# Fourteen squarings of a power iteration, taken out of the first attention scores and dealt between the matmuls that enter the first batch

## The chip, the core and the metric

The kernel runs on one core of one Trainium2 chip. The metric is the device time of one execution in microseconds, the median of several runs. The engines that matter here are TensorE (PE in the profile; PEld is its weight load), VectorE (DVE), ScalarE (ACT), GpSimd (POOL) and SyncE (SP), which issues the DMAs. Each of them works through an instruction stream of its own, and the streams meet at semaphores.

## What is computed

The input is x, 8 images of 512 channels and 32 x 32 pixels, in float32. Four layers follow each other; each ends with the addition of its own input. Cut to what matters:

```python
# layer 0: attention whose scores are divided by their largest singular value
f = relu(batchnorm(conv1x1(x, Wf)));  g = relu(batchnorm(conv1x1(x, Wg)));  h = conv1x1(x, Wh)
z = einsum('bcn,bcm->bnm', f, g)
attn = z / svd(z)[..., 0]
x = conv1x1(einsum('bnm,bcm->bcn', attn, h), Wv) + x
# layer 1: group norm, softmax attention over 512 channels, projection
hn = group_norm(x);  q, k, v = Wq hn, Wk hn, Wv hn
x = x + Wp (softmax(q k / sqrt(512)) v)
# layer 2: softmax attention over 128 channels, projection, batch norm with given statistics
# layer 3: sign(x + b) times signed weights, batch norm, two slopes
```

The largest singular value of z in layer 0 need not come from the 1024 x 1024 matrix z itself: z is a product of f and g with 64 channels each, so its singular values follow from the 64 x 64 Gram matrices of f and of g. The kernel squares the product of the two Gram matrices again and again and reads the largest eigenvalue off traces.

## The kernel before, in words

**Pairs and chains.** Two images make a pair. Their 64-channel Gram matrices stand as two diagonal blocks of one 128 x 128 matrix, so one matmul serves two images. The function chain(j, split) works on pair j. It is a Python generator: each call of next() issues one step and stops at the next yield. A chain has 22 steps. Step 1 multiplies the Gram matrices; in each of steps 2 to 21 the current matrix cur is multiplied with itself. products issues two 128 x 128 matmuls for that (lines 1022 and 1023), one for the matrix and one for its transpose. evict then copies both from PSUM to the next cur: in a plain step ACT does it (L1036), in a step with a trace DVE does it and scales by the reciprocal of the trace (L1042 in step 1, L1044 later). A trace is taken from the diagonal (diagonal, L1049 and L1050, on DVE), summed over the partitions by a matmul with a mask (total, L1054 on PE), copied (L1055) and inverted (L1062 or L1077). Traces are taken in step 1, then in steps 5, 8, 11, 14, 17 and 20, and two at once in step 22. Step 2 of a chain also holds a power on POOL (L1067) and four small DVE instructions (L1068 to L1071) that take a root of the first trace. Step 22 holds no squaring; it ends with a logarithm and an exponential on ACT (L1098 and L1101), each with a table load, and scales the pair's matrix on DVE (L1105). After it the pair is ready.

**Four chains.** The pair that is worked on first (images 6 and 7) has its chain in the early part of the kernel. The other three chains are one generator after the other, called behind, with 66 steps in all. In the main loop, chore(2) takes one step of behind at every second call.

**Entry of an image.** enter adds layer 0's result to x. It makes four visits for the first image, two for each later one. In a visit of the first image, PE makes two 64-row matmuls into two PSUM banks (L411), and DVE adds them to x (L420), takes statistics (L423) and joins them (L425). After the visits, the group norm follows: a small matmul over groups (L432), some small DVE instructions, a second small matmul (L439), and then a reciprocal square root and scale and bias (L233 to L238, with a power on POOL at L234, then L442 to L445). Then normal writes the normalised image h (L462), split_h forms differences of its quarters (L326 to L329), and make_u starts layer 1's first products (L387), which need them. For the first image all of L462 is on DVE.

**Fillers.** The early part has other matmuls to do that wait for little: transposes, Gram matrices (L1335) and products of weights (L1281). filler is a generator of such pieces, called todo. While the first image enters, they are dealt out between the steps of the entry: weights0 first (L289), then four visits, then the two halves of the group norm, seven dealings in all.

**Order.** In the early part the order of PE's instructions is the order in which the program writes them (a manual schedule for that engine). DVE, ACT and POOL are ordered by the compiler's scheduler from estimates. Each engine's order is fixed when the program is compiled.

**PSUM.** In the early part there are two wide tiles and four banks. The visits, the chain steps, the traces and the two small matmuls share the four banks. In the main loop there are eight banks.

**The main loop.** fast(env, n, hb, ua) handles image n in a fixed order: scores1 (28 steps of seven products, with exponentials), make_v, values1, and then layers 2 and 3. The next image enters inside scores1. Chores are skipped at a few k so that they don't meet a visit:

```python
            if k in (10, 13, 20, 27):
                next(ahead, None)
            if not rest3 and k not in (13, 14, 15, 20, 21, 22):
                chore(2)
```

scores1 of image 0 thus makes 11 of the calls, make_v and values1 seven each, 25 together; image 1 makes 23 because layer 3 of image 0 still runs at its start, and image 2 makes the last 18.

Of the kernel before, what the change touches and what calls it, by code (L numbers as in the profile page):

```python
# [85 lines left out]
def kernel(  # L86
# [772 lines left out]
    def entering(n):  # L859

        b = order[n]
        f = load_f(b)

        def steps():
            while b // 2 not in ready:
                next(behind)
            if b % 2 == 0:
                for i in (b, b + 1):
                    pvs[i] = weights0(i)
            yield  # L870
            yield from enter(resident[b], f, pvs.pop(b), 2 if n else CC)

        return steps()
# [244 lines left out]
    def chains():  # L1118
        for j in rest:
            yield from chain(j, False)  # L1120

    behind = chains()
# [238 lines left out]
    def relu(b, i):  # L1361
        t = (fs, gs)[i][b]
        nc.scalar.activation(t, t, AF.Relu, bias=bi0[:, i : i + 1], scale=sc0[:, i : i + 1])
        if i == 0:
            nc.sync.dma_start(out=f_dram[b], in_=t)
# [82 lines left out]
    with tc.manual_schedule(engines={mybir.EngineType.PE}):  # L1448
        steps = entering(0)
        for k, _ in enumerate(chain(jl, True)):  # L1450

            for _ in range(4 if k == 3 * NSTEP + 3 else 2 if k != 1 and k % 3 < 2 else 1):
                next(todo, None)
            for args in (next(relus, None),):
                if args:
                    relu(*args)
        for n in (2, 3, 3, 3, 3, 4, 6):
            next(steps)
            for _ in range(n):
                next(todo, None)  # L1460
        for _ in todo:
            pass
    early.close()
# [192 lines left out]
```

## Time and profile before

| what | value |
|---|---|
| median of 3 runs | 1911.45 us (1911.01 to 1911.63) |
| profiled execution, its own time | 1911.79 us |
| its span | 1909.9 us, 16334 instructions |
| granted TensorE clock | 0.998 |
| first visit's L411 | at 165.94 us |
| the other three visits' L411 | at 169.84, 173.67 and 177.50 us |
| L432, L439 | at 182.02 and 185.78 us |
| L462 (h) | from 188.89 us, 3.74 us long |
| first exponential of L365, images 0 to 3 | at 226.67, 449.26, 670.92 and 888.84 us |
| first exponential of L365, images 4 and 5 | at 1098.85 and 1307.62 us |

Times inside the profile count from the span's start. The span is a little shorter than the execution's own time; what lies around it is not in the trace. PE's 32-bit matmuls appear as two records each, so that "x4" stands for two of them. Ends of matmuls are modelled, and successive records overlap; the distance between starts is the better measure of what a matmul costs. The stretch from one image's first exponential to the next one's is a period of the main loop. The periods of images with an even and an odd number differ a little, because weights0 is made for two images at once.

What one loop chain leaves in the trace before: it starts at 220.20 us, with step 1, and its steps lie about 4 us apart inside scores1.

### The profile page before, as it was taken

To read this page: it belongs to the slowest core of one execution; us is meant where nothing else is said; L and a number is where in the kernel's file an instruction comes from. 1 tells how busy PE (TensorE), PEld (TensorE's weight loads), DVE (VectorE), ACT (ScalarE), POOL (GpSimd) and SP (SyncE) were. 2 spreads that over 40 slices of the span, in tenths; PEclk is the share of its full clock that TensorE was granted. 3 is DMA by queue.
4 is the path that set the end of the run, shared out by engine and by line. 5 is a ranking of instruction groups with operands and counts; after the bars stand their busy time and mean duration, and the time that the engine had idled before them with its cause. 6 is when DMAs were issued, how large, how long until landed. Compare 5 with 4: busy or idle time off the path is not lost.

```text
span 1909.9 us, 16334 instructions
## 1 busy us (share of the span) xinstructions
PE 1886.4 (99%) x6118; PEld 977.5 (51%) x6118; DVE 1130.2 (59%) x1762; ACT 510.3 (27%) x811; POOL 224.5 (12%) x176
## 2 busy tenths in 40 slices
PE   9999999999999999999999999999999999999997
PEld 4366456544745447444645446544645455544653
DVE  3256676448664677447664676457753775466547
ACT  2142121134212332035202431034202521234014
POOL 0000011201121011200121011201120011101121
PEclk9999999999999999999999999999999999999999
DMA  8420000002000120002000120002000200010001
GB/s 320 159 78 6 0 6 12 1 12 88 17 1 0 34 72 12 1 11 88 17 1 0 38 68 12 0 13 87 11 1 9 91 12 0 1 34 22 12 0 46
DMA packets 27782, 66.45 MB, mean 35 GB/s; under 512 B 4272, under 2 KB 5424, under 8 KB 27056
## 3 DMA queue, kind: packets, MB, share of 16 engines
q1 hardware_dynamic: 26768, 64.90, 10.1%
q8 instruction: 50, 0.82, 0.2%
q10 hardware_dynamic: 864, 0.43, 0.1%
q14 instruction: 36, 0.29, 0.1%
q0 software_dynamic: 64, 0.00, 0.0%
HBM read 38.51 MB, written 18.87 MB: 30 GB/s over the span
## 4 chain that ended last, share of the span: by engine, by line
PE 92%; DVE 7%; issue 1%; ACT 1%; DMA 0%; POOL 0%; DVEq 0%; ACTq 0%
PE bank L387 42%; PE bank L556 20%; PE bank L951 6%; PE bank L805 6%; PE bank L1241 5%; PE bank L657 3%; PE bank L411 2%; PE bank L674 2%; DVE both L748 1%; DVE both L718 1%; PE wide L1281 1%; PE wide L1335 1%; PE bank L1022 1%; PE bank L1023 1%; PE bank L697 1%; PE bank L826 1%
## 5 line engine op out<-in xcount | busy, mean ns | idle before, releaser
L556 PE MATMUL bank<-e,vt 128*128 128x512 f32 x768 | 334.2, 593 | 0.0
L556 PEld LDWEIGHTS bank<-e,vt 128*128 128x128 f32 x768 | 144.9, 190 | 174.8 <-issue 173.2
L387 PE MATMUL bank<-ut,h 128*128 128x512 f32 x384 | 182.3, 597 | 0.0
L344 DVE TENSOR_TENSOR e<-bank,e 128x512 f32<-128x512 f32 x128 | 87.8, 686 | 81.9 <-PE bank L387 80.8
L387 PE MATMUL bank<-us,hs 128*128 128x512 f32 x256 | 121.5, 597 | 1.3 <-DVE us L316 0.5
L387 PEld LDWEIGHTS bank<-ut,h 128*128 128x128 f32 x384 | 71.4, 190 | 95.6 <-issue 84.0
L951 PE MATMUL bank<-e,tpg 128*128 128x512 f32 x256 | 114.7, 595 | 0.0
L805 PE MATMUL bank<-tpg 128*128 128x512 f32 x256 | 114.6, 592 | 0.0
L812 ACT ACTIVATE e<-bank 128x512 f32<-128x512 f32 x128 | 76.4, 597 | 128.6 <-PE bank L805 128.6
L387 PE MATMUL bank<-h,wu 128*128 128x512 f32 x192 | 90.4, 593 | 2.4 <-DVE h L462 1.7
L387 PE MATMUL bank<-wo,h 128*128 128x256 f32 x384 | 91.8, 382 | 0.0
L817 DVE TENSOR_TENSOR esum<-esum,e 128x1024 f32<-128x1024 f32 x48 | 58.8, 1225 | 54.9 <-ACT e L812 54.9
L359 POOL TENSOR_TENSOR e<-e 128x512 f32<-128x512 f32 x32 | 43.4, 1356 | 403.8 <-ACT e L338 238.3
L951 PEld LDWEIGHTS bank<-e,tpg 128*128 128x128 f32 x256 | 48.1, 190 | 63.2 <-issue 63.1
L805 PEld LDWEIGHTS bank<-tpg 128*128 128x128 f32 x256 | 48.6, 190 | 60.7 <-issue 60.5
L387 PEld LDWEIGHTS bank<-wo,h 128*128 128x128 f32 x384 | 71.6, 190 | 13.5 <-ACT vt L338 4.1
L359 POOL TENSOR_TENSOR ut<-ut 128x512 f32<-128x512 f32 x16 | 21.7, 1359 | 476.1 <-ACT ut L340 476.1
L344 DVE TENSOR_TENSOR vt<-bank,vt 128x512 f32<-128x512 f32 x64 | 44.1, 689 | 56.2 <-PE bank L387 55.8
L387 PEld LDWEIGHTS bank<-us,hs 128*128 128x128 f32 x256 | 47.1, 190 | 54.9 <-issue 48.3
L834 DVE RECIPROCAL rsum<-bank 128x512 f32<-128x512 f32 x15 | 50.4, 3358 | 38.2 <-PE bank L826 38.2
L685 ACT ACTIVATE sg<-xt,rb 128x512 f16<-128x512 f32 x64 | 45.0, 718 | 103.7 <-DVE xt L676 100.2
L1241 PE MATMUL bank<-xt,fg 128*64 128x512 f32 x256 | 59.5, 613 | 4.6 <-DMA fg<-in_w_fg 4.6
(330 smaller groups left out, 3017.2 us busy)
## 6 DMA issues: line engine op xcount, KB each, us to landing
xt<-in_x SPq DMA_DIRECT2D x55, 512.0 KB
out<-both SPq DMA_DIRECT2D x63, 256.0 KB
rfull<-rsum SPq DMA_DIRECT2D x60, 128.0 KB
f_dram<-f SPq DMA_DIRECT2D x8, 256.0 KB
fb<-f_dram SPq DMA_DIRECT2D x8, 256.0 KB
w<-in_w SPq DMA_DIRECT2D x1, 1024.0 KB
q<-in_w_q SPq DMA_DIRECT2D x1, 1024.0 KB
k<-in_w_k SPq DMA_DIRECT2D x1, 1024.0 KB
```

Of the source, the lines that this page charges most:

```text
L344: nc.vector.tensor_tensor(dst, ps, u, ALU.add)
L359: nc.gpsimd.tensor_tensor(c22, c22, c12, ALU.add)
L387: mm(out=ps[:, q * w : (q + 1) * w], lhsT=lt(ka, kb, q, k), rhs=rhs(ka, kb, q, k), start=first and q == 0 and k == 0, stop=last and k == 1 ...
L556: mm(out=ps, lhsT=a[:, t, bass.ts(r_, P)], rhs=e[t], start=first and t == 0, stop=last and t == NTH - 1, skip_group_check=True,)
L657: mm(out=ps[:, i, :], lhsT=xt[:, cc, bass.ts(4 * h + i, P)], rhs=sbw["tpg"][:, cc, 2 * P : 3 * P], start=cc == 0, stop=cc == CC - 1,)
L685: nc.scalar.activation(sg[:, cc, :], xt[:, cc, half(h)], AF.Sign, bias=rb3[:, cc : cc + 1])
L805: mm(out=ps, lhsT=pt[:, 0, bass.ts(t, P)], rhs=tt[:, 0, half(h)], start=True, stop=True,)
L812: nc.scalar.activation(e[:, half(h)], ps, AF.Exp, scale=float(P) ** -0.5)
L817: nc.vector.tensor_tensor(esum, esum, e, ALU.add)
L834: nc.vector.reciprocal(r, ps)
L951: mm(out=banks[h], lhsT=gt[:, t, :], rhs=es[t][:, half(h)], start=t == 0, stop=t == NT - 1,)
L1241: mm(out=banks[i][side(h), :], lhsT=w0[i][:, cc, :], rhs=xt[:, cc, half(h)], start=cc == 0, stop=cc == CC - 1,)
```

## The change

The seven dealings of the first entry get 2, 2, 3, 3, 3, 3 and 4 fillers instead of 2, 3, 3, 3, 3, 4 and 6, and after each of the first two fillers of a dealing one step of behind is taken. That makes 14 steps: 1 to 14 of the chain of the pair that comes next. Fillers that are left over come after the last dealing, as before.

```diff
-        for n in (2, 3, 3, 3, 3, 4, 6):
+
+        for n in (2, 2, 3, 3, 3, 3, 4):
             next(steps)
-            for _ in range(n):
+            for i in range(n):
                 next(todo, None)
+                if i < 2:
+                    next(behind)
         for _ in todo:
             pass
```

The generator behind was in the program before and isn't changed; its later steps are still taken by chore in the main loop. On PE, the compiled order of the changed program has, per dealing, a filler, a squaring, a filler, a squaring, and the rest of the fillers. On DVE, the instructions of these steps now stand between those of the visits and of the group norm: step 5's L1044, for example, behind the last L423 and L425 of the second visit, and all of step 14's (L1049, L1050, L1055, L1077, L1044) between L445 and L462. On ACT, the copies of the plain steps stand before and between the two copies of L1294. The three chains end earlier in the main loop: in scores1 of images 0, 1 and 2 instead of in their values1.

## The prediction

> **What bounds the kernel now.** I read the page first, for the busy shares.
>
> ```profile
> PE 1886.4 (99%) x6118; PEld 977.5 (51%) x6118; DVE 1130.2 (59%) x1762; ACT 510.3 (27%) x811; POOL 224.5 (12%) x176
> ```
>
> TensorE (PE) is the bound almost everywhere, so work taken off PE in one place pays only if its new place holds PE idle time. Two views settle this: the busy time by stretch and PE's waits. The stretches run from one image's first exponential at L365 to the next one's. Columns are length, then busy time of PE, weight loads, VectorE (DVE), ScalarE (ACT), GpSimd (POOL):
>
> ```profile
> 449.26:670.92 221.66, 221.54 (x719) 117.40 (x718) 138.56 (x229) 64.23 (x107) 27.60 (x20) 1.00 0.08 25
> 670.92:888.84 217.92, 217.81 (x687) 114.28 (x686) 135.24 (x211) 62.27 (x101) 25.71 (x19) 1.00 0.08 26
> 888.84:1098.85 210.01, 209.90 (x613) 105.73 (x612) 127.02 (x176) 56.27 (x87) 26.56 (x19) 1.00 0.09 27
> 1098.85:1307.62 208.77, 208.66 (x609) 105.51 (x608) 126.33 (x175) 55.70 (x87) 26.59 (x19) 1.00 0.08 27
> ```
>
> PE is never idle in the main loop, and chain steps are paid for in full: n=2 takes 217.92 us where n=4, the same work without chain steps, takes 208.77; n=1 takes 221.66 against 210.01 for n=3. PE's waits from 160 to 200 us show the idle time that the first image's entry leaves (waited for, us, times, longest):
>
> ```profile
> PE bank L387 <- DVE h L462: 1.7, 1, 1.7
> PE bank L387 <- DVE hs L327: 0.9, 1, 0.9
> PE bank L387 <- ACT ut L349: 0.7, 1, 0.7
> PE bank L432 <- DVE mv L431: 0.6, 1, 0.6
> ```
>
> That is 3.9 us in all, three of the four waits at its end. The chain of waits there (start, us, what) shows whose path it is:
>
> ```profile
> 182.41 3.54 PE wide L1281 x8
> 185.94 0.13 PE bank L439 x2
> ...
> 186.34 1.03 POOL r_r L234
> ...
> 188.90 3.73 DVE h L462 x8
> 192.63 1.15 DVE hs L326
> 193.80 1.24 DVE hs L327
> 195.04 0.04 issue
> 195.08 19.35 PE bank L387 x44
> ```
>
> From L439 to 195.08 the end is set by DVE, with one GpSimd power; before L439, by PE and its fillers. So a microsecond put before L439 on PE, or anywhere on DVE after it, moves everything. Last, the timeline of one chain step as the loop runs it (start, us, engine, line):
>
> ```profile
> 235.95 0.38 PE L1022 MATMUL bank<-cur 128*128 128x128 f32 x2
> 236.17 0.39 PE L1023 MATMUL bank<-cur 128*128 128x128 f32 x2
> 236.39 0.28 PE L1054 MATMUL bank<-tj,mask 128*128 128x1 f32 x2
> 236.76 0.15 DVE L1055 COPY tr<-bank 128x1 f32<-128x1 f32 x1
> 236.94 0.17 DVE L1077 RECIPROCAL r<-tr 128x1 f32<-128x1 f32 x1
> 237.14 0.54 DVE L1044 TENSOR_SCALAR cur<-bank,r 128x256 f32<-128x256 f32 x1
> ```
>
> The next squaring needs this cur, so a step with a trace is followed by products at the earliest 237.68 - 235.95 = 1.73 us after its own, even with every engine free. A plain step is evicted by ACT (L1036, 0.37 us): in the same trace L1023 starts at 124.34 and its ACT copy at 124.82, so its successor may start about 0.22 + 0.48 + 0.37 = 1.1 us after it.
>
> [...] in the entry, DVE sits idle 2.90 us before L233 with later work behind it. [...] the trace has 1.28 us twice per chain end (L1098, L1101)[...].
>
> **The change, part by part.** No DMA moves, SP's order is unchanged, and no computation is added. 14 of the 66 calls of the three loop chains go from the loop into the entry: steps 1 to 14 of chain 0, two for each of the seven dealings, with traces in steps 1, 5, 8, 11 and 14. Fillers are the same matmuls; two of them now end after the last dealing.
>
> *Removed from the loop.* The loop makes 25 calls in n=0, 23 in n=1 and 18 in n=2. With 14 fewer to do, n=0 and n=1 make as many as before, of later steps, and n=2 makes 4. The price per step: n=1 (221.66 - 210.01) / 23 = 0.507 us; n=2 (217.92 - 208.77) / 17 (one of the 18 lies ahead of the stretch) = 0.538; over both 20.8 / 40 = 0.52. Removed: 14 x 0.52 = 7.3 us, bounds 7.0 and 7.5. All of it is on the path, since PE has no gap there.
>
> *Added to the entry, PE alone.* Four matmul records take 0.45 us, a trace 0.12: 14 x 0.45 + 5 x 0.12 = 6.9 us. If only that counted, the 3.3 us of idle PE behind L439 would hide steps 13 and 14, and the entry would grow by 3.6 to 6.0 us.
>
> *Added to the entry, the hand-overs.* The steps lie one filler apart (0.87 to 0.89 us of PE: four fillers are the 3.54 us of the chain above), and the compiled order of the changed program fixes where DVE does its part. I follow both queues on the clock of the profile, starting at L289 (162.62), with a visit's DVE work as in the trace: L420, L423, L420, L423 in 2.9 us from 1.16 us after L411, L425 0.2.
> Step 1: L1054 starts 165.47, L1055 165.79, but L1068 stands ahead of L1042 in DVE's queue and waits for the power at L1067 (0.56 us in the loop, 1.0 at worst). Cur is there at 167.2, PE was ready at 166.57: 0.6 us lost. First L411: 167.7 (before 165.94). Steps 2 to 4 fit: second L411 171.6 (169.84).
> Step 5, the costliest: DVE has L420, L423, L420, then L1055, then L423, L1077, L425 and only then L1044. The second visit's DVE work begins at 172.9, so cur is there at 176.95; PE wanted it at 174.97 for step 6. Lost: 2.0 us. Third L411: 178.3 (173.67).
> Step 8: L1054 waits for L1050, which stands behind the third visit's last L423 and L425 (183.1), while its products ended at 182.0. Lost: 1.1 us. Fourth L411: 184.4 (177.50). Steps 9 and 10 fit, though ACT evicts step 10 only behind its 1.0 us copy at L1294: L432 188.9 (182.02).
> Step 11: 1.7 us of hand-over against 1.4 us of PE: 0.3 us lost. L439 193.0 (185.78).
> After L439 DVE needs 2.65 us to the end of L445, as before: 196.0 (188.75). Then its queue holds step 14's L1049, L1050, the wait for PE's L1054, L1055, L1077 and L1044 ahead of the memset and of L462: 0.3 + 0.3 + 0.45 + 0.18 + 0.2 + 0.54 = 2.0 us more. L462 starts at 198.15 instead of 188.89. Everything queued behind it on DVE (h, hs) and PE's L387 shift with it.
> Entry: +9.25 us. Both ends: 6.0 if DVE's share hides, 10.5 with the slow power and 0.92 us for each filler (the chain of waits has 2.77 for three).
>
> *Moved within the loop.* The three chain ends (two table loads, ln, exp, L1105) move from the values stages (n=0, 1, 2) to the score stages, k=18, 16 and 11, next to entry visits that take four PSUM banks at once. Before, they cost PE nothing visible: the only PE gap in the loop to 760 us is 0.5 us at 217.85. In the score stage DVE is held about 2 us and ACT 3 to 4 us; with eight banks I take 0.5 us for all three together, bounds 0 and 4.5 (1.5 us each).
>
> Sum: 9.25 - 7.3 + 0.5 = +2.45 us. The profiled run took 1911.79 us (span 1909.9), 0.34 above the median of 1911.45; the sum on it gives 1914.2, and on the median 1913.9. I predict 1913.9 us, 0.13% above before, which within 0.2% (3.8 us, about what a measurement of this kernel can tell) is no change.
>
> **Rivals.**
> *A, the entry absorbs the steps.* DVE's and ACT's parts hide and only PE counts: 3.6 - 7.3 = -3.7 us, 1907.7; with DVE's end part half hidden about 1909. For it: DVE is busy 15.6 of the 26 us from 163 to 189. Against: its queue is in order, and four stalls come out of fixed positions. Chance 0.12, half of it beyond -0.2%.
> *B, chain ends beside entry visits stall PE.* One mechanism: at k=18 (n=0), 16 and 11 the score stage runs out of free banks while DVE waits for ACT's second table load; the visit at k=20 or 13 then waits. It decides from about 0.5 us a time; at 1.5 us each the time is 1911.45 + 9.25 - 7.3 + 4.5 = 1917.9. For it: a visit needs four of the eight banks. Against: a bank is wanted again only some 12 us later (an estimate: seven products of four records, about 1.75 us each in the trace). Chance 0.20.
> *C, the loop does not get shorter.* The steps in n=2 were hidden work and 7.3 us does not come back: 1911.45 + 9.25 = 1920.7. Against: the 9 us between two images alike. Chance 0.04.
> The forecast has 0.64; its own range is 1911.5 to 1916.2.
>
> **How the numbers follow.** Faster by over 0.2% (below 1907.6): half of A, 0.06. Slower by over 0.2% (above 1915.3): B and C nearly whole, 0.21, and 0.09 of the forecast's upper end: 0.30. Within: 0.64. The range reaches down to A's middle, 1909.3, and up to B, 1918.0.
>
> **What would show it.** The stretch of n=2 should fall from 217.92 to about 210.5, n=1 stay within 0.5 of 221.66. PE should wait about 2 us at L1022 for DVE's L1044 (step 6), about 1 us at L1054 for L1050 (step 8), and L462 should start near 198. If L462 starts before 195, A holds; gaps of PE over 0.5 us between 226 and 760 mean B; n=2 above 216 means C.

## The result, and the profile after

The changed kernel takes 1914.05 us (median of 20 runs, 1913.02 to 1914.53) against 1910.8 us for the kernel before in the same runs (20 runs, 1909.93 to 1911.63). The ratio is 1.0016, with a 95% interval of 1.0009 to 1.0022: slower by 3.25 us by the medians (1.7 to 4.2 by the interval), and within the 0.2% that the prediction called no change. The profiled execution has a span of 1911.3 us, on the same clock as before (0.998).

The first view is again the busy time by stretch, from one image's first exponential to the next one's (length, then busy time of PE, weight loads, DVE, ACT, POOL). Image 0's stretch in the kernel before:

```profile
226.67:449.26 222.59, 222.47 (x721) 118.27 (x720) 139.29 (x227) 63.16 (x103) 25.88 (x19) 1.00 0.05 13
```

Images 0, 1 and 2 in the changed kernel:

```profile
233.88:458.15 224.27, 222.97 (x723) 118.41 (x722) 140.94 (x232) 62.72 (x102) 26.63 (x19) 1.00 0.04 13
458.15:679.80 221.65, 221.54 (x717) 117.28 (x716) 138.22 (x225) 63.80 (x106) 26.20 (x20) 1.00 0.08 25
679.80:890.38 210.58, 210.46 (x622) 107.04 (x621) 129.84 (x190) 59.19 (x93) 26.53 (x19) 1.00 0.08 27
```

Image 2's stretch fell from 217.92 to 210.58 us: the loop's saving, 7.34 us. Image 1's is unchanged. Image 0's grew from 222.59 to 224.27, by 1.68 us. PE is not busy in 1.3 us of it (224.27 - 222.97), where it was not busy in 0.1 us before.

The second view is PE's waits from 155 to 205 us (waited for, us, times, longest):

```profile
PE bank L1054 <- DVE tj L1050: 1.3, 2, 0.7
PE bank L1022 <- DVE cur L1044: 1.2, 2, 1.0
PE bank L387 <- DVE hs L327: 0.9, 1, 0.9
...
PE bank L387 <- ACT ut L349: 0.7, 1, 0.7
PE bank L1022 <- DVE half__1277 L1069: 0.6, 1, 0.6
```

The two waits of L387 that the kernel before had are still there, of the same size: the idle time before the differences hs was not filled. Its waits before L432 and for the first h are gone, and 3.0 us of new waits for DVE stand in the entry. One of them, in the timeline (start, us, engine, line):

```profile
172.88 0.28 PE L1054 MATMUL bank<-tj,mask 128*128 128x1 f32 x2
...
173.62 0.15 DVE L1055 COPY tr<-bank 128x1 f32<-128x1 f32 x1
173.74 0.69 DVE L423 BATCH_NORM_STATS2 st<-xt 128x6 f32<-128x512 f32 x1
174.35 0.15 DVE L1077 RECIPROCAL r<-tr 128x1 f32<-128x1 f32 x1
174.47 0.21 DVE L425 BATCH_NORM_AGGREGATE mv<-st 128x2 f32<-128x12 f32 x1
174.60 0.49 DVE L1044 TENSOR_SCALAR cur<-bank,r 128x256 f32<-128x256 f32 x1
175.14 0.49 PE L1022 MATMUL bank<-cur 128*128 128x128 f32 x2 [1.01 <-DVE cur L1044]
```

Step 5's trace is on its way, but in DVE's queue its reciprocal (L1077) stands behind a statistic of the image (L423) and its eviction (L1044) behind the joining of the statistics (L425), so step 6 starts 1.01 us after PE was free. L1077 started 0.58 us after the end of L1055, whose result it takes (173.77 to 174.35), with L423 between them; in step 8, with nothing between them, it started 0.03 us after it (181.81 to 181.84). The end of the entry, in the chain of waits (start, us, what):

```profile
194.24 0.16 DVE bi L445
194.41 0.21 DVE diag L1049
194.62 0.02 issue
194.64 0.30 DVE tj L1050
194.94 0.14 issue
195.08 0.37 PE bank L1054 x2
195.44 0.02 issue
195.47 0.17 DVE tr L1055
195.64 0.02 issue
195.66 0.17 DVE r L1077
...
196.54 3.52 DVE h L462 x8
```

Between L445 and L462 the path that sets the end now runs through step 14's trace, which nobody needs before the loop takes step 15. L462 starts at 196.46 us by the timeline, 35.22 us after the first L289, where it started 26.27 us after it before: the entry grew by 8.95 us.

The sum of the profiled executions: +8.95 (L289 to L462), -0.36 (L462 to the first exponential), +1.68 (image 0), -0.01 (image 1), -7.34 (image 2), -0.1 (the rest) = +2.8 us, of the 3.25 us measured. What lies before L289 doesn't belong to the change: it took between 161.2 and 162.9 us in all the profiled executions of this study. In this trace 1.1 of the 1.4 us are there by the end of PE's first 32 matmul records (the next group starts at 12.95 us, at 14.08 in the trace before), in front of everything that the change moves.

### The profile page after: what moved, and what is told of

Its sections match the earlier page's. It is cut to its first block, busy times and chain, and to the rows that moved or that the text cites. A ratio compares the mean times of both kernels' runs of the same rounds, so it can differ in the third digit from the quotient of the medians.

```text
span 1911.3 us, 16343 instructions
## 1 busy us (share of the span) xinstructions
PE 1886.3 (99%) x6118; PEld 974.4 (51%) x6118; DVE 1130.7 (59%) x1762; ACT 510.1 (27%) x811; POOL 224.5 (12%) x176
## 4 chain that ended last, share of the span: by engine, by line
PE 91%; DVE 7%; issue 1%; ACT 1%; DMA 0%; POOL 0%; DVEq 0%; ACTq 0%
PE bank L387 41%; PE bank L556 20%; PE bank L951 6%; PE bank L805 6%; PE bank L1241 4%; PE bank L657 3%; PE bank L674 2%; PE bank L411 2%; DVE both L748 1%; DVE both L718 1%; PE wide L1335 1%; PE bank L1022 1%; PE wide L1281 1%; PE bank L1023 1%; PE bank L697 1%
## 5 line engine op out<-in xcount | busy, mean ns | idle before, releaser
L387 PE MATMUL bank<-ut,h 128*128 128x512 f32 x384 | 182.2, 597 | 0.0
L344 DVE TENSOR_TENSOR e<-bank,e 128x512 f32<-128x512 f32 x128 | 87.9, 687 | 72.4 <-PE bank L387 70.5
L387 PE MATMUL bank<-us,hs 128*128 128x512 f32 x256 | 121.5, 597 | 1.4 <-DVE us L316 0.5
L387 PEld LDWEIGHTS bank<-ut,h 128*128 128x128 f32 x384 | 71.4, 190 | 95.6 <-issue 85.2
L387 PE MATMUL bank<-wo,h 128*128 128x256 f32 x384 | 91.9, 382 | 0.0
L387 PE MATMUL bank<-h,wu 128*128 128x512 f32 x192 | 90.3, 593 | 0.7 <-ACT ut L349 0.7
L359 POOL TENSOR_TENSOR e<-e 128x512 f32<-128x512 f32 x32 | 43.5, 1358 | 396.2 <-ACT e L338 233.7
L344 DVE TENSOR_TENSOR vt<-bank,vt 128x512 f32<-128x512 f32 x64 | 44.1, 689 | 59.1 <-PE bank L387 58.7
L387 PEld LDWEIGHTS bank<-wo,h 128*128 128x128 f32 x384 | 71.6, 190 | 14.3 <-ACT vt L338 4.9
L359 POOL TENSOR_TENSOR ut<-ut 128x512 f32<-128x512 f32 x16 | 21.7, 1359 | 477.9 <-ACT ut L340 477.9
L387 PEld LDWEIGHTS bank<-us,hs 128*128 128x128 f32 x256 | 47.2, 190 | 55.9 <-issue 49.0
L657 PEld LDWEIGHTS bank<-tpg,xt 128*128 128x128 f32 x512 | 59.5, 192 | 7.2 <-issue 7.2
```

The costliest lines, as they stand in the source:

```text
L344: nc.vector.tensor_tensor(dst, ps, u, ALU.add)
L359: nc.gpsimd.tensor_tensor(c22, c22, c12, ALU.add)
L387: mm(out=ps[:, q * w : (q + 1) * w], lhsT=lt(ka, kb, q, k), rhs=rhs(ka, kb, q, k), start=first and q == 0 and k == 0, stop=last and k == 1 ...
L657: mm(out=ps[:, i, :], lhsT=xt[:, cc, bass.ts(4 * h + i, P)], rhs=sbw["tpg"][:, cc, 2 * P : 3 * P], start=cc == 0, stop=cc == CC - 1,)
```

## The experiments

Each was measured beside the kernel before, on the same chip. The columns after the ratio are from each one's profiled execution: the starts of L439, and of L327 (the difference that releases the second part of the first products), counted from the first L289; the stretches of images 0, 1 and 2; and the time from the first L289 to the end of the span, against before. This last column ("by the traces" below) leaves out what differs ahead of the first L289. It is one execution each, to about 0.1 us, and it helps to compare kernels with each other where their intervals against before overlap.

| kernel | against before, us | ratio (95%) | L439 | L327 | image 0 | image 1 | image 2 | L289 to end |
|---|---|---|---|---|---|---|---|---|
| before | 0 | | 23.16 | 31.18 | 222.59 | 221.66 | 217.92 | 0 |
| changed | +3.25 | 1.0016 (1.0009 to 1.0022) | 30.21 | 40.00 | 224.27 | 221.65 | 210.58 | +2.8 |
| e1_fillers_alone | -1.81 | 0.9990 (0.9982 to 0.9999) | 21.44 | 29.46 | 222.59 | 221.66 | 217.92 | -1.6 |
| e2_steps_old_dealing | +4.27 | 1.0024 (1.0015 to 1.0032) | 32.26 | 41.31 | 224.27 | 221.65 | 210.57 | +4.3 |
| e3_thrown_away | +8.60 | 1.0045 (1.0031 to 1.0058) | 30.21 | 40.01 | 222.59 | 221.65 | 217.92 | +9.1 |
| e4_thirteen | +1.52 | 1.0008 (1.0000 to 1.0017) | 30.20 | 38.59 | 222.59 | 223.31 | 211.02 | +2.2 |
| e5_one_each | -2.11 | 0.9988 (0.9981 to 0.9995) | 24.18 | 32.56 | 222.59 | 221.87 | 214.13 | -2.3 |
| e6_steps_apart | +0.63 | 1.0004 (0.9996 to 1.0013) | 27.98 | 37.88 | 224.26 | 221.67 | 210.56 | +0.9 |
| e8_late_fillers | -3.71 | 0.9981 (0.9973 to 0.9988) | 18.92 | 27.04 | 222.59 | 221.66 | 217.91 | -4.0 |
| e9_skip_k18 | +4.08 | 1.0022 (1.0013 to 1.0031) | 30.21 | 39.99 | 223.01 | 222.07 | 212.43 | +3.7 |
| e10_five_steps | -3.81 | 0.9980 (0.9972 to 0.9987) | 21.57 | 29.69 | 222.82 | 221.66 | 215.25 | -3.9 |

**The two parts alone.** The new dealing without squarings, against the kernel before:

```diff
-        for n in (2, 3, 3, 3, 3, 4, 6):
+        for n in (2, 2, 3, 3, 3, 3, 4):
```

> Only the new dealing of the fillers (2, 2, 3, 3, 3, 3, 4), no squarings in the entry. Hand-over theory (VectorE's in-order queue and the matmuls of the steps set what the entry grows by): the dealing itself helps a little, since L439 comes after two fillers fewer, so L439 and L462 are 1.0 to 1.7 us earlier after L289 than before (23.2 and 26.3 us) and the time is 1.0 to 1.7 us below before. Rival, the dealing is what costs: 2 to 3 us above before. Rival, only the matmuls of the steps count: within 0.5 us of before.

L439 came 1.72 us earlier and the time fell by 1.81 us, just beyond the upper end of what was expected. And the squarings with the old dealing, against the changed kernel:

```diff
-        for n in (2, 2, 3, 3, 3, 3, 4):
+        for n in (2, 3, 3, 3, 3, 4, 6):
```

> The 14 squarings in the entry, with the fillers dealt out as before (2, 3, 3, 3, 3, 4, 6). Hand-over theory: the two parts add up; the old dealing puts two fillers more ahead of L439 and so costs the 1.7 us that the fillers alone gained: L439 30.2 + 1.7 = 31.9 us after L289, the time 1.0 to 1.9 us above the changed kernel, so 4.2 to 5.2 above before. Rival, the old dealing gives the steps more room and their waits shrink: equal to the changed kernel or below it.

L439 came 2.05 us later than in the changed kernel, and the time against before is 1.0 us higher (1.5 by the traces), within what was expected: part of the delay came back behind L439, where the trace of step 14 now fell between parts of L462 (L327 is only 1.31 us later). So the two halves of the change pull against each other: the dealing alone gains 1.8 us, and the moved squarings alone, with what the loop gets back, cost 4.3 us.

**The entry priced by itself.** The 14 steps in the entry belong to an extra chain that is never finished; the loop keeps its 66 calls.

```diff
+        spare = chain(rest[0], False)
...
-                    next(behind)
+                    next(spare)
```

> The changed entry, but its 14 steps belong to an extra chain that is then abandoned; the loop keeps all its 66 calls, as before. This prices the entry by itself. Hand-over theory: L462 starts 35 us after L289, as in the changed kernel, the stretches of images 0, 1 and 2 stay at 222.6, 221.7 and 217.9 us, and the time is 8.6 us (7.5 to 9.5) above before. Rival, only the matmuls of the steps count and the loss of the change is made in the loop: 4 to 6 us above before.

L462 starts 35.24 us after L289, and the time is 8.6 us above before (9.1 by the traces), so the rival that made the loop responsible, 4 to 6 us above before, falls. The loop's stretches are those of the kernel before:

```profile
234.51:457.10 222.59, 222.47 (x721) 118.26 (x720) 139.27 (x227) 63.08 (x103) 25.88 (x19) 1.00 0.04 13
678.75:896.67 217.92, 217.81 (x687) 114.27 (x686) 135.23 (x211) 62.24 (x101) 25.70 (x19) 1.00 0.08 26
```

**The hand-overs.** The same 14 steps and the same fillers, but the second step of a dealing stands after its last filler.

```diff
-                if i < 2:
+                if i in (0, n - 1):
                     next(behind)
```

> The changed kernel with the same 14 steps and the same fillers, but the second step of each dealing stands after its last filler instead of after its second, so that two or more fillers or a visit lie between any two steps. Hand-over theory: the waits of 1.0 us at step 6 and of 0.65 at step 8 and 0.15 at step 12 go, for no other change in the work of either engine; VectorE's share ahead of the end stays (step 14's trace now falls between the parts of L462). L439 comes 1.5 us or more earlier (28.7 us after L289 instead of 30.2), and the time is 1.0 to 1.8 us below the changed kernel, 1.2 to 2.2 above before. Rival, the steps' own matmuls are the price: no change against the changed kernel, 3.2 above before.

PE's waits from 160 to 205 us in that run:

```profile
PE bank L387 <- DVE hs L327: 1.9, 1, 1.9
PE bank L387 <- ACT ut L349: 0.7, 1, 0.7
PE bank L1022 <- DVE half__1277 L1069: 0.6, 1, 0.6
PE bank L1022 <- DVE cur L1044: 0.2, 1, 0.2
```

L1054's waits are gone, L1022's wait for L1044 fell from 1.2 to 0.2 us, and step 2's wait, whose neighbours didn't move, kept its 0.6. L439 came 2.23 us earlier, and the time is 2.6 us below the changed kernel by the medians, 1.9 by the traces, where 1.0 to 1.8 were expected. The gaps that went ahead of L439 make 1.66 us of the 2.23; a gap understates its wait, as the next section shows, and what else came with the new order was not priced. No matmul and no VectorE instruction was saved (6118 and 1762 records in both traces); only the distances between the steps, and with them the order of the queues, changed.

**Fewer steps.** Step 14 left to the loop, and in another kernel one step per dealing, seven in all:

```diff
-        for n in (2, 2, 3, 3, 3, 3, 4):
+        for d, n in enumerate((2, 2, 3, 3, 3, 3, 4)):
...
-                if i < 2:
+                if i < 2 - (d == 6):
```

> As the changed kernel, but step 14, the one whose trace stands between L445 and L462 on VectorE, stays in the loop. Hand-over theory: L462 starts 2.0 us earlier after L289 than in the changed kernel (33.2 instead of 35.2), the loop gives back 0.5 us, and the first chain ends one call later (k=23 instead of 18), where its wait of 1.2 us at L1054 may go: the time is 1.5 to 2.8 us below the changed kernel, so 0 to 1.7 above before. Rival, only the matmuls of the steps count: step 14 was hidden in TensorE's idle time behind L439, so 0.5 us above the changed kernel, 3.5 above before.

```diff
-                if i < 2:
+                if i < 1:
```

> One step per dealing, seven in all, a whole dealing apart, with traces in steps 1 and 5 only. Hand-over theory: TensorE loses 0.6 us at step 2 and nothing at the other steps, no trace stands ahead of L462, so the entry grows by 3.4 us of matmuls and 0.6 us, less the 0.45 us of step 7 and the 1.0 to 1.7 us of the dealing: about 2.2 us; the loop saves 7 x 0.52 = 3.6 us; the time is 1.4 us (0.5 to 2.5) below before. Rival, each step costs in the entry what it cost in the changed kernel (9 us for 14): the entry grows by 4.5 us and the time is 0.9 us above before.

With 13 steps, L327 came 1.41 us earlier and L462 1.48, not the expected 2.0: the timeline has step 14's L1049 and L1050 still between L445 and L462, 0.6 us, because the program issues the diagonal at the end of step 13. What went is the round trip to PE and back. Image 0's stretch is back at 222.59, but image 1's grew by 1.65 us, so that the time is 1.7 us below the changed kernel by the medians and only 0.6 by the traces. PE's waits in that run name the same pair of lines as in the changed kernel, in the other image:

```profile
PE bank L1054 <- DVE td L1050: 1.2, 1, 1.2
```

In both, it is the call at k=18 that takes the last step of a chain: in the changed kernel the eighth call of image 0, here the sixth of image 1. With seven steps the chains end outside the score stage and no stretch grew like that. There L439 is 1.0 us later than before, where with the fillers alone it was 1.7 us earlier. So the seven steps cost 2.7 us ahead of L439 and 3.1 by L327, and the loop got back 3.6 us (217.92 + 221.66 less 214.13 + 221.87). The time fell by 2.11 us, most of which the fillers alone had given.

**The place k=18.** In the changed kernel, the loop skips k=18 too.

```diff
-            if not rest3 and k not in (13, 14, 15, 20, 21, 22):
+            if not rest3 and k not in (13, 14, 15, 18, 20, 21, 22):
```

> The changed kernel, with k=18 added to the calls at which the loop takes no chain step, so that the first chain's last step, whose trace matmul waited 1.2 us for VectorE at k=18, is taken at k=19. If that place costs the 1.7 us by which image 0's stretch grew, the stretch falls from 224.3 to about 222.6 us and the time is 1.2 to 1.8 us below the changed kernel, 1.4 to 2.0 above before. Rival, the end of a chain in the score stage costs this wherever it falls: no change, 3.2 above before.

The wait at L1054 went, as expected, and image 0's stretch fell by 1.26 us, of which about 0.5, by the price of a step, is the call that it no longer makes. The time did not fall: it is 0.8 us above the changed kernel (0.9 by the traces). One skipped place per image moves other steps to other places, and image 2 now makes six calls instead of four. PE's waits in the loop and the entry of that run, among others:

```profile
PE bank L1022 <- DVE cur L1042: 1.2, 2, 0.6
...
PE bank L387 <- DVE e L344: 0.5, 1, 0.5
```

So the wait is tied to the place. But new waits came in its stead: 0.6 us for the first eviction of a chain (L1042) in each of images 0 and 1, and 0.5 us for L344 in image 2. They took more than the skipped place gave. The expectation for the whole time was wrong.

**The fillers again.** If L439 only waits for fillers, the fillers can go behind it, where DVE works alone. No squarings; against the kernel before:

```diff
-        for n in (2, 3, 3, 3, 3, 4, 6):
+        for n in (2, 2, 3, 2, 4, 1, 6):
```

> No squarings in the entry; fillers dealt 2, 2, 3, 2, 4, 1, 6: one filler fewer in the third visit, one more in the fourth, where TensorE waited for VectorE, one between L432 and L439 instead of three, and six after L439, where VectorE works alone. If the entry's length is set by the fillers ahead of L439 and by VectorE after it, L439 comes about 2.3 us earlier than with the fillers alone (19.1 us after L289 instead of 21.4) and TensorE has idle time enough behind it: 3.4 to 4.4 us below before. If TensorE's own work is the bound there, no better than the fillers alone: 1.8 us below before.

3.71 us below before. L439 came 2.52 us earlier than with the fillers alone. Of PE's waits from 160 to 205 us one is left:

```profile
PE bank L387 <- ACT ut L349: 0.7, 1, 0.7
```

With one step in each of the first five dealings besides:

```diff
-        for n in (2, 3, 3, 3, 3, 4, 6):
+        for d, n in enumerate((2, 2, 3, 2, 4, 1, 6)):
             next(steps)
-            for _ in range(n):
+            for i in range(n):
                 next(todo, None)
+                if i < 1 and d < 5:
+                    next(behind)
```

> The fillers of the run with six late fillers, and one chain step in each of the first five dealings (two with a trace). Theory: with the fillers dealt so, TensorE has next to no idle time left in the entry that a squaring could fill, so that a step moved there pays 0.45 us to save 0.52, and step 2 still loses 0.6 us: the time is within 0.7 us of the run with late fillers, 3 to 4.4 us below before. Rival, steps in the entry are worth their 0.52 us each if they don't wait: 2.6 us below that run, 6 below before.

1907.19 us against 1907.57 with the late fillers alone, each beside its own runs of before (-3.81 and -3.71): no difference. Either one beats both the kernel before and the changed one. That is what was expected: with the late fillers, PE's only wait left in the entry is the 0.7 us for L349, in both runs, so there was next to no idle time that the steps could fill.

## Why the prediction was right

The predicted 1913.9 us and +2.45 us stand against 1914.05 us and +3.25 (+2.8 by the traces). The mechanism was right: the loop gives back its price, and the entry pays more than that, by PE's own work ahead of L439, by hand-overs in DVE's queue and by DVE's work behind L445. That the sum came so close is partly luck, because several terms were off in opposite directions. Step by step:

- **Removed from the loop: right.** 14 steps at 0.52 us were to bring 7.3 us; image 2's stretch fell by 7.34 and image 1's stayed. The run with the abandoned chain shows the same saving as missing there.
- **Added to the entry: right as a sum, 8.95 us against 9.25, and right in its cause.** L439 was predicted 7.2 us later and came 7.05 later. The prediction said that L462 would start near 198; it starts at 196.46, or 197.8 with the 1.4 us by which this execution's L289 came earlier.
- **Single terms of it were mis-sized, and cancelled.** Step 2 lost 0.56 us as predicted (0.6). Step 6 lost 1.01 instead of 2.0, because DVE worked through its queue faster (L1044 done 3.5 us after the visit's first L420, not 4.05) and PE was ready later; step 8 lost 0.65 instead of 1.1, step 12 0.15 instead of 0.3: 2.4 us of gaps in all where 4.0 were predicted. Two things made up for it. A gap understates its wait: a matmul record of 512 columns is shown 0.59 us long, but its successor normally starts after 0.43, and at step 6 it starts 1.61 us after, which is 1.18 late for a gap of 1.01, so by the distances between starts the four waits cost about 3.0 us. And 0.87 us for a filler was too little: beside a visit's matmul, or behind the norm's or a trace's, an L1281 filler takes 0.94 to 1.04 us to the next start, and 0.86 only beside other fillers or between squarings.
- **After L439: right.** 2.0 us more were predicted between L445 and L462 and 1.9 were measured. What was missed is that only the round trip belongs to step 14: its diagonal is issued by step 13.
- **Moved within the loop: mis-sized.** The term "0.5 us for all three together" measured 1.68, all of it in image 0, none in images 1 and 2. By the sign that the prediction gave for it, a PE gap of over 0.5 us in the loop, rival B came true at one of its three places, k=18 in image 0, but not by the means that it named, a shortage of banks while DVE waits for a table load: PE waits at the trace matmul itself, for a DVE that is at work, and the first table load (L1098, 1.28 us, at 263.32) begins while it does. The timeline of the changed kernel there:

```profile
262.07 1.27 POOL L359 TENSOR_TENSOR e<-e 128x512 f32<-128x512 f32 x1 [14.40 <-DVE e L344]
262.16 0.29 DVE L1050 TENSOR_REDUCE td<-diag 128x1 f32<-128x128 f32 x1
262.48 1.00 DVE L1049 TENSOR_TENSOR diag<-cur 128x128 f32<-128x128 f32 x1
...
263.52 0.29 DVE L1050 TENSOR_REDUCE td<-diag 128x1 f32<-128x128 f32 x1
...
263.86 0.38 PE L1054 MATMUL bank<-td,mask 128*128 128x2 f32 x2 [1.19 <-DVE td L1050]
```

Step 21's matrix was in place at 259.70 (ACT's copy), but DVE's queue has its diagonals behind parts of a visit and of a score until 261.84, and the second diagonal takes 1.00 us instead of its usual 0.29. L1054 starts 1.78 us after the last L387 record in front of it, where 0.43 is usual: 1.35 of the 1.68 us. The rest was not traced to one place.
- **The rivals.** A (the entry absorbs the steps) is refuted by e3_thrown_away, C (the loop gets no shorter) by image 2's stretch. That the fillers' dealing was the loss, a rival of the experiments, is refuted by e1_fillers_alone: it is a gain.

What stays open: about 0.5 us between the sum of the traces and the medians, which is within the interval. The slow diagonal at k=18 was not tested by itself; the last section has what the traces show of it.

## What to carry to other kernels

Moving work off a saturated engine into another stretch pays only for the idle time that it really fills there: here a step cost 0.52 us in the loop and about 0.75 in the entry. That is L327's delay against the kernel with the new dealing alone, 40.00 - 29.46 = 10.5 us, over 14 steps; the entry's own growth, 8.95 us, hides what the new dealing gained. Before moving anything, see what sets the end of the target stretch; the idle time lay behind L439, and taking fillers from in front of that instruction, which is no added work at all, brought 3.7 us, where the whole move lost 3. A chain of steps that hands over between engines belongs where two of its steps are farther apart than a hand-over takes in the receiving engine's queue as it is filled there; what it takes when that engine is free is too little: step 6's products came 2.70 us after step 5's (172.44 to 175.14), where the prediction's 1.73 us counts on free engines, and with the steps farther apart PE's waits for L1044 fell from 1.2 to 0.2 us. And its work should not stand in front of the one instruction that everything waits for: step 14's trace and eviction there took 1.9 us more between L445 and L462.

## What was unexpected of the hardware

- A filler's two records start 0.43 us apart, and the next matmul 0.43 us later. Next to a matmul with 64 rows (L411), or behind one with one to four columns (L432, L439, L1054), one of the two distances is 0.51 to 0.53 us instead, in both kernels alike. Each such neighbour costs nearly a tenth of a microsecond, and no view shows it as a wait. In the changed kernel, a filler behind a visit takes 0.96 us to the next start, and one between squarings 0.86:

```profile
177.71 1.13 PE L1281 MATMUL wide<-p,nat_v 128*128 128x512 f32 x2
...
178.67 0.38 PE L1022 MATMUL bank<-cur 128*128 128x128 f32 x2
...
179.11 1.02 PE L1281 MATMUL wide<-p,nat_v 128*128 128x512 f32 x2
...
179.97 0.38 PE L1022 MATMUL bank<-cur 128*128 128x128 f32 x2
```

- The diagonal at L1049 multiplies two tiles of 128 x 128. All 36 in the trace before take 0.23 to 0.29 us, and so do 34 of the 36 in the changed kernel's; the other two take 1.00 us (at 262.48, the one at k=18) and 1.35 us (at 551.26). Both started while POOL was adding 128 x 512 elements (L359 and L595) and ended 0.15 us after the addition did, and no other L1049 of the two traces started during such an addition. In e4_thirteen one of 1.00 us (at 484.41) and in e9_skip_k18 one of 1.01 us (at 263.93) also started during an L359 and ended 0.15 us after it. Two lines of the changed kernel away from k=18:

```profile
550.29 2.18 POOL L595 TENSOR_TENSOR xt<-xt,o_b 128x512 f32<-128x512 f32 x1 [1.83 <-DVE o_b L593]
...
551.26 1.35 DVE L1049 TENSOR_TENSOR diag<-cur,ident 128x128 f32<-128x128 f32 x1
```

A small POOL instruction did not go with a slow diagonal: in each of the two traces an L1049 started inside the 1.02 us of a power on 128 x 4 elements (L234) and took 0.29 us (at 731.09 before, at 519.15 after). By the trace, the slow diagonal makes 0.7 of the 1.2 us that PE waited at k=18 (1.00 - 0.29 us). No run took the POOL addition away, so that the addition is the cause was not shown.
